# Two idle TensorE products at the start, and VectorE sums in the first three steps of a four-layer attention chain

## The chip, the cores and the metric

The kernel runs on one core of a Trainium2 chip. TensorE multiplies matrices into PSUM, VectorE (DVE in the profile) and ScalarE (ACT) read PSUM and work between PSUM and SBUF, GpSimd (POOL) does small work, and the sync engine (SP) issues most DMAs. The metric is device time in microseconds, the median of several runs.

## The reference

Four layers are applied in a row to `x` of shape (4, 64, 64, 64), all in float32. Every layer is an attention of 4096 tokens with 64 channels per image. The change touches layer 0 of the first image, which computes

```
q = x @ Wq + bq;  k = x @ Wk + bk;  v = x @ Wv + bv       # per image: 4096 x 64
attn = softmax(q @ k.T, axis=-1)                          # 4096 x 4096, rows sum to 1
out  = attn.T @ v                                         # note the transpose
x    = gamma * out + x
```

Layer 1 is an attention over max-pooled keys with spectrally normalised weights, layers 2 and 3 are attentions after a group norm. They are not touched.

## The kernel before

**Work and order.** `fast_path` writes all work in one order by hand (manual scheduling): every engine runs its instructions in the order in which the Python code issues them. The unit is a `step`. In a step of layer 0, `first` runs twice: each makes one score tile of 128 query rows by 1024 keys (TensorE, line 999, into one of two rotating PSUM buffers `s`) and its exponential on ScalarE. Four score tiles make one block of 128 query rows. Three steps later the products with the values follow (`adds`, line 1028). Between these, `step` calls `advance`, which lets a background generator issue its next piece: projections, values, constants, or parts of another layer. `now[0]` counts the steps since the start of the kernel; layer 0 of the first image has steps 0 to 63.

**The fold of the query and key weights.** The scores are x A x^T with A = Wq Wk^T, so only one projected tensor is needed, in two arrangements called `q` and `q_swapped`; the keys are the transposed input `xT` itself.

**The start.** Before step 0 the code issues, for TensorE in this order: two idle products (`keep_busy`, line 703: zeros times zeros, 128 by 256, into a score buffer that nobody reads), the transposes of Wq and Wk (line 730), one idle product, the product A (line 736), the transposes of the first half of the input (line 930, evacuated by VectorE at line 870 and ScalarE at line 878, one half each), the product for the bias (line 740), one idle product, and the first halves of the two projections (line 891, evacuated at lines 872 and 880). Each float32 product shows as two passes in the profile.

**Steps 0 to 2.** The background pieces are, in step 0, the transposes of the second half of the input, again evacuated by VectorE and ScalarE; in steps 1 and 2, the two halves of the values (line 912, into a score buffer, evacuated with the bias by VectorE at line 916). In a step the two calls of `first` are issued ahead of the background piece:

```python
        if first is not None:
            first()                  # both score tiles, both exponentials
        work = due.pop(now[0], [])   # empty in steps 0 to 2
        ...
        if len(work) < 2:
            advance(MID)             # the background piece
```

**The row sums.** The softmax needs the sum of each exponential's rows. `first` has two ways for it: ScalarE's accumulator beside the exponential (line 1009), or an exponential without it (line 1006) and a sum on VectorE (line 1007). It takes the second where the background waits at a place called `LATE` or `END`, which in layer 0 happens for a part of the second image. After the fourth tile of a block, VectorE adds the four columns (line 1011) and takes the reciprocal (line 1012); ScalarE scales the values with it (line 1017) from step 3 on.

Of the kernel before, what the change touches and what calls it, by code (L numbers as in the profile page):

```python
# [597 lines left out]
def fast_path(tc: tile.TileContext, a: dict, out: bass.AP, bad, read_flag):  # L598
# [9 lines left out]
    nc = tc.nc  # L608
# [3 lines left out]
    P = 128  # L612
# [7 lines left out]
    MID, ALONE, LATE, END = range(4)  # L620
# [8 lines left out]
    s_tile = lambda: ps_s.tile([P, 1024], FP, tag="s", name="s")  # L629
# [67 lines left out]
    idle = scratch[:, 12 * P : 16 * P]  # L697
    nc.vector.memset(idle, 0.0)

    def keep_busy(n):  # L700

        for _ in range(n):
            nc.tensor.matmul(s_tile()[:, 0:256], idle[:, 0:P], idle[:, 0:256], start=True, stop=True)

    load_form(0, 0, a["L0_conv_Wq"], a["L0_conv_Wk"])
    load[:] = [nc.sync.dma_start]
# [27 lines left out]
    def form_product(n, t):  # L734

        nc.tensor.matmul(t, form[n][2][:, 0, :], form[n][2][:, 1, :], start=True, stop=True)
# [5 lines left out]
    def form_scaled(n, i, t, factor):  # L742
        nc.vector.tensor_scalar(blocks[n][i], t, factor, None, ALU.mult)
# [12 lines left out]
    def check_columns(n):  # L756
        i = checks[0]
        checks[0] += n
        return all_z[:, i : i + n], all_r[:, i : i + n]
# [16 lines left out]
    now = [0]  # L776
# [3 lines left out]
    back = {"gen": iter(()), "at": None, "credit": 0.0, "tempo": 1.0, "alone": -1}  # L780
# [35 lines left out]
    def step(first=None):  # L816
        back["credit"] = min(back["credit"] + back["tempo"], 3.0)
        for f in before.pop(now[0], ()):
            f()
        if first is not None:  # L820
            first()
        work = due.pop(now[0], [])
        for n, f in enumerate(work[:2]):
            if n == 1:
                advance(MID)
            split = n == 1 and ready(LATE)
            f(lambda: advance(LATE)) if split else f()
        for f in work[2:]:
            f()
        if len(work) < 2:  # L830
            advance(MID)
            advance(LATE)
        passes = list(later)
        later.clear()
        for f in passes:
            f()
        advance(END)
        now[0] += 1
# [7 lines left out]
    def parts(within, whole):  # L846

        if within is None or whole:
            yield slice(0, 512)
            if within is not None:  # L850
                within()
        else:
            yield slice(0, 256)
            within()
            yield slice(256, 512)

    def banks(on):

        if on == "both" and now[0] < 2:
            bank = [acc_tile(), acc_tile()]  # L860
            return bank, bank
        s = s_tile()
        bank = [s[:, chunk(i)] for i in range(2)]
        return bank if on == "both" else s, bank

    def evacuate(on, dst, src, bias=None):

        if on == "DVE":
            if bias is None:
                nc.vector.tensor_copy(dst, src)  # L870
            else:
                nc.vector.tensor_scalar(dst, src, bias, None, ALU.add)
        elif on == "both":
            m = dst.shape[-1] // 2
            evacuate("DVE", dst[:, 0:m], src[0], bias)
            evacuate("ACT", dst[:, m:], src[1], bias)
        elif bias is None:
            nc.scalar.copy(dst, src)
        else:
            nc.scalar.activation(dst, src, AF.Identity, bias=bias)  # L880
# [42 lines left out]
    def transposed(on, st):  # L923
        xin = st.pop("xin")
        xT = st["x"] = x_tile("xT")
        for g in range(2):
            yield MID
            s, bank = banks(on)
            for i in range(8):
                nc.tensor.transpose(bank[i // 4][:, ds(i % 4 * P, P)], xin[:, g * 8 + i, :, :].rearrange("p i c -> p (i c)"), ident)  # L930
            evacuate(on, xT[:, wide(g)], s)
# [24 lines left out]
    def first_queries(st):  # L956

        st["q"] = x_tile("q"), x_tile("q_swapped")
        st["v"] = x_tile("v").rearrange("p (j f) -> p j f", f=C)
        A, col = blocks[0]  # L960
        st["todo"] = [project("both", q, A, st["x"], col, exchanged=n == 1) for n, q in enumerate(st["q"])]
        for g in st["todo"]:
            next(g)
        yield from first_half(st)
# [13 lines left out]
    def layer0(st):  # L978

        q, k, v = st.pop("q"), st["x"], st.pop("v")
        pairs = NB * NC // 2
        acc, ps, zs, scaled = {}, {}, {}, {}
        zsum, rz = check_columns(NB)

        def queries(m, i, e):

            c, n = divmod(m // 2, 4)
            return q[(c + i) % 2][half(i), ds(c // 2 * 1024 + m % 2 * 512 + n * P + e * C, C)]  # L990

        def first(u):
            m, c = divmod(u, NC)
            if c == 0:
                zs[m] = small.tile([P, NC], FP, tag="z0", name="z0")
            s = s_tile()
            for i in range(2):
                for e in range(2):
                    nc.tensor.matmul(  # L999
                        s[half(e), chunk(i)], queries(m, i, e), k[half(i), chunk(c)], start=True, stop=True  # L1000
                    )
            p = ps[u] = p_tile()
            z = zs[m][:, c : c + 1]
            if back["at"] in (LATE, END):

                nc.scalar.activation(p, s, AF.Exp)
                nc.vector.tensor_reduce(z, p, AX.X, ALU.add)
            else:
                nc.scalar.activation(p, s, AF.Exp, accum_out=z)  # L1009
            if c == NC - 1:  # L1010
                nc.vector.tensor_reduce(zsum[:, m : m + 1], zs.pop(m), AX.X, ALU.add)  # L1011
                nc.vector.reciprocal(rz[:, m : m + 1], zsum[:, m : m + 1])

        def scale(t):
            m = 2 * t // NC
            vs = scaled[t] = z_p.tile([P, C], FP, tag="vs", name="vs", bufs=1)
            nc.scalar.activation(vs, v[:, m, :], AF.Copy, scale=rz[:, m : m + 1])  # L1017

        def add(t, e, n, cols):

            m, second = divmod(2 * t, NC)
            c = (second + 2 * e) % NC + n
            if c not in acc:
                acc[c] = acc_tile()
            for i in range(2):
                nc.tensor.matmul(  # L1028
                    acc[c][half(i), cols], scaled[t][half(e), :], ps[NC * m + c][half(e), chunk(i)][:, cols],
                    start=(m == 0 and not second), stop=(m == NB - 1 and second > 0),  # L1030
                )
                yield

        def adds(t, n, within=None):
            for cols in parts(within, t * 2 < NC or t >= pairs - NC // 2):
                for row_tiles in zip(add(t, 0, n, cols), add(t, 1, n, cols)):
                    pass
            if n == 1:
                del scaled[t]
                if t % 2:  # L1040
                    for u in range(2 * t - 2, 2 * t + 2):
                        ps.pop(u)

        def finish(cs):
            xT = st["x"]
            for c in cs:
                nc.vector.scalar_tensor_tensor(xT[:, chunk(c)], acc.pop(c), gamma0, xT[:, chunk(c)], ALU.mult, ALU.add)
            if not acc:
                st["done0"] = True

        start = now[0]
        for t in range(pairs):
            g = start + t + 3
            before.setdefault(g, []).append(lambda t=t: scale(t))
            due.setdefault(g, []).extend([lambda *within, t=t, n=n: adds(t, n, *within) for n in range(2)])
        due[start + pairs + 2].append(lambda: finish((0, 2, 1, 3)))
        for t in range(pairs):
            step(lambda: (first(2 * t), first(2 * t + 1)))
        return start + pairs + 3
# [516 lines left out]
    def alone(*phases):  # L1576
        background(1.0, *phases)
        drain()

    s0, s1, s2, s3 = state  # L1580
    def rest(phase):
        yield MID
        yield from phase

    keep_busy(2)
    form_transposes(0, s_tile())
    keep_busy(1)
    t = s_tile()[:, 0:P]
    form_product(0, t)
    form_scaled(0, 0, t, 1.0)  # L1590
    st0 = transposed("both", s0)
    next(st0)
    next(st0)
    t = s_tile()[:, 0:1]
    form_bias(0, t)
    form_scaled(0, 1, t, 1.0)
    keep_busy(1)
    alone(first_queries(s0))


# [59 lines left out]
    at = 10 * C  # L1660
# [227 lines left out]
```

## Time and profile before

| What | Value |
|---|---|
| Runs | 2926.57, 2926.76, 2927.2 us |
| Median | 2926.76 us |
| Profiled execution, from the first to the last instruction | 2927.0 us (the page names no other time for it) |
| TensorE matmul busy | 2895.3 us, 99% |
| VectorE busy | 1871.5 us, 64% |
| ScalarE busy | 1800.3 us, 62% |
| Mean granted TensorE clock | 0.998 |

Times are microseconds from the first instruction. In the profile PE is TensorE's matmul, PEld its weight load; a line such as L999 is a line of the kernel. An arrow `out<-in` names the tiles, and a bracket behind a row of the timeline gives the idle time before it and what ended it. "xcount" merges several instructions into one row.

### The profile page before, as it was taken

What the parts mean: (1) busy time and instruction counts of PE and PEld (TensorE: products, weight loads), DVE (VectorE), ACT (ScalarE), POOL (GpSimd) and SP (SyncE); (2) the same over time, 40 slices, a digit from 0 to 9 for tenths busy, and PEclk for the clock granted to TensorE, in tenths of its full rate; (3) what the DMA queues carried; (4) which work ended last, traced back from release to release, by engine and by line L of the source; (5) the groups of instructions that cost most, each with busy time, mean ns of one, the idle gap of its engine ahead of it and who ended that gap; (6) DMA issues with size and microseconds to landing.
All of it is one profiled execution on the core that took longest, in us unless ns stands there. A gap on an engine that the chain in (4) does not pass through costs nothing.

```text
span 2927.0 us, 66546 instructions
## 1 busy us (share of the span) xinstructions
PE 2895.3 (99%) x29397; PEld 1113.6 (38%) x29397; DVE 1871.5 (64%) x2141; ACT 1800.3 (62%) x2481; POOL 35.2 (1%) x35
## 2 busy tenths in 40 slices
PE   9999999999999999999999999999999999999998
PEld 3333233333444433344443343333344444443333
DVE  2111753589821078963027897888888877878878
ACT  5666666665566766566766655555555655555554
POOL 0000000000000000000000000000000000000000
PEclk9999999999999999999999999999999999999999
DMA  2010000000001000000000000000000000000000
GB/s 38 1 30 7 1 1 16 7 5 5 19 5 30 1 7 5 5 23 16 1 1 7 5 9 19 19 5 9 5 19 8 20 5 8 6 20 5 8 5 10
DMA packets 85513, 30.64 MB, mean 10 GB/s; under 512 B 79168, under 2 KB 83264, under 8 KB 83808
## 3 DMA queue, kind: packets, MB, share of 16 engines
q1 hardware_dynamic: 83168, 25.87, 4.8%
q8 instruction: 232, 3.80, 0.6%
q10 hardware_dynamic: 1984, 0.38, 0.1%
q14 instruction: 65, 0.53, 0.1%
q0 software_dynamic: 64, 0.07, 0.0%
HBM read 4.79 MB, written 4.19 MB: 3 GB/s over the span
## 4 chain that ended last, share of the span: by engine, by line
PE 97%; DVE 1%; ACT 1%; issue 0%; DMA 0%; POOL 0%; ACTq 0%; DVEq 0%
PE acc L1323 30%; PE s L1288 30%; PE s L999 15%; PE acc L1028 15%; PE s L1122 2%; PE acc L1148 2%; ACT p L1128 1%; DVE zacc L1299 1%; PE s L1148 1%; PE s L891 0%; PE s L912 0%; PE s L1419 0%; PE s L1467 0%; PE s L1092 0%; PE s L1194 0%
## 5 line engine op out<-in xcount | busy, mean ns | idle before, releaser
L1293 ACT ACTIVATE p<-s 128x1024 f32<-128x1024 f32 x1024 | 994.6, 1022 | 696.2 <-PE s L1288 676.5
L1299 DVE TENSOR_TENSOR zacc<-zacc,p 128x1024 f32<-128x1024 f32 x960 | 1174.2, 1223 | 179.7 <-ACT p L1293 114.8
L1323 PE MATMUL acc<-p,v 64*64 64x512 f32 (+1 forms) x8576 | 1006.6, 573 | 0.0
L1009 ACT ACTIVATE p<-s 128x1024 f32<-128x1024 f32 x480 | 487.3, 1020 | 114.8 <-PE s L999 114.6
L1323 PEld LDWEIGHTS acc<-p,v 64*64 64x64 f32 x8576 | 340.4, 133 | 545.1 <-issue 545.1
L1028 PE MATMUL acc<-p,vs 64*64 64x512 f32 (+1 forms) x4224 | 501.4, 577 | 0.0
L1288 PE MATMUL s<-q,k 64*64 64x512 f32 x2048 | 491.6, 590 | 2.1 <-ACT p L1128 2.1
L999 PE MATMUL s<-xT,q 64*64 64x512 f32 x2048 | 487.2, 591 | 2.4 <-DVE mean L1355 0.7
L1288 PE MATMUL s<-q,xT 64*64 64x512 f32 x2048 | 489.5, 591 | 0.0
L999 PE MATMUL s<-xT,q_swapped 64*64 64x512 f32 x2048 | 487.6, 591 | 0.3 <-DVE o L1157 0.3
L1288 PE MATMUL s<-q,h_swapped 64*64 64x512 f32 x2048 | 481.0, 591 | 3.9 <-DVE v L916 3.5
L1288 PE MATMUL s<-q,k_swapped 64*64 64x512 f32 x2048 | 480.4, 590 | 0.0
L1011 DVE TENSOR_REDUCE all_z<-z 128x1 f32<-128x4 f32 x128 | 20.1, 157 | 606.5 <-ACT p L1009 606.2
L1028 PEld LDWEIGHTS acc<-p,vs 64*64 64x64 f32 x4224 | 173.3, 133 | 266.0 <-issue 264.2
L1288 PEld LDWEIGHTS s<-q,h_swapped 64*64 64x64 f32 x2048 | 145.5, 133 | 144.5 <-issue 131.7
L1288 PEld LDWEIGHTS s<-q,k_swapped 64*64 64x64 f32 x2048 | 148.1, 133 | 137.6 <-issue 87.2
L999 PEld LDWEIGHTS s<-xT,q_swapped 64*64 64x64 f32 x2048 | 146.2, 133 | 141.8 <-issue 110.3
L1288 PEld LDWEIGHTS s<-q,xT 64*64 64x64 f32 x2048 | 145.7, 133 | 138.1 <-issue 131.7
L999 PEld LDWEIGHTS s<-xT,q 64*64 64x64 f32 x2048 | 144.2, 133 | 139.3 <-issue 110.8
L1288 PEld LDWEIGHTS s<-q,k 64*64 64x64 f32 x2048 | 148.6, 133 | 116.7 <-issue 96.2
L1017 ACT ACTIVATE vs<-v,all_r 128x64 f32<-128x64 f32 x256 | 89.1, 348 | 157.2 <-PE acc L1028 80.3
L1128 ACT ACTIVATE p<-s 128x1024 f32<-128x1024 f32 x128 | 124.1, 1022 | 82.4 <-PE s L1122 78.5
(213 smaller groups left out, 1319.6 us busy)
## 6 DMA issues: line engine op xcount, KB each, us to landing
k_swapped<-k SPq DMA_DIRECT2D x8, 512.0 KB, 5.8
residual<-turned SPq DMA_DIRECT2D x128, 32.0 KB, 1.9
h_swapped<-xT SPq DMA_DIRECT2D x8, 512.0 KB, 5.3
out_dram<-turned SPq DMA_DIRECT2D x60, 64.0 KB, 2.0
xin<-in_x_dram SPq DMA_DIRECT2D x12, 256.0 KB, 6.8
q_swapped<-q SPq DMA_DIRECT2D x6, 512.0 KB, 5.5
pg<-pg SPq DMA_DIRECT2D x8, 128.0 KB, 2.3
xin<-in_x_dram SPq DMA_DIRECT2D x12, 64.0 KB, 2.4
```

Source lines behind the costliest of these rows:

```text
L999: nc.tensor.matmul(s[half(e), chunk(i)], queries(m, i, e), k[half(i), chunk(c)], start=True, stop=True)
L1009: nc.scalar.activation(p, s, AF.Exp, accum_out=z)
L1011: nc.vector.tensor_reduce(zsum[:, m : m + 1], zs.pop(m), AX.X, ALU.add)
L1017: nc.scalar.activation(vs, v[:, m, :], AF.Copy, scale=rz[:, m : m + 1])
L1028: nc.tensor.matmul(acc[c][half(i), cols], scaled[t][half(e), :], ps[NC * m + c][half(e), chunk(i)][:, cols], start=(m == 0 and not second) ...
L1122: nc.tensor.matmul(ss[e][half(m), chunk(i)], pgs[0 if e == d else 1][r, ds(n * P + m * C, C)], th[r, chunk(i ^ j)], start=True, stop=True,)
L1128: nc.scalar.activation(pk[e], ss[e], AF.Exp)
L1148: nc.tensor.matmul(acc[quarter(q), :], g[:, k, :], ps[j, k][q // 2][:, chunk(q % 2)], start=(k == 0 or not bank), stop=(k == NK - 1 or not ...
L1288: nc.tensor.matmul(s[half(e), chunk(i)], k[(j + i) % 2][half(i), ds(j // 2 * P + e * C, C)], q[half(i), chunk(c)], start=True, stop=True,)
L1293: nc.scalar.activation(p, s, AF.Exp)
L1299: add = lambda: nc.vector.tensor_tensor(zaccs[c], p0, p, ALU.add)
L1323: nc.tensor.matmul(accs[c][e][half(i), cols], v[half(e), j, :], p[half(e), chunk(i)][:, cols], start=(j == 0), stop=(j == NB - 1),)
```

## The change

The idle product ahead of the first projection is left out. A shorter one, of 128 columns, is put between the product A and the transposes of the input. And in the steps 0, 1 and 2 (six score tiles), the row sums are made by VectorE instead of ScalarE's accumulator.

```diff
-    def keep_busy(n):
+    def keep_busy(n, cols=256):
 
         for _ in range(n):
-            nc.tensor.matmul(s_tile()[:, 0:256], idle[:, 0:P], idle[:, 0:256], start=True, stop=True)
+            nc.tensor.matmul(s_tile()[:, 0:cols], idle[:, 0:P], idle[:, 0:cols], start=True, stop=True)
...
             z = zs[m][:, c : c + 1]
-            if back["at"] in (LATE, END):
+            if back["at"] in (LATE, END) or now[0] < 3:
 
                 nc.scalar.activation(p, s, AF.Exp)
                 nc.vector.tensor_reduce(z, p, AX.X, ALU.add)
             else:
                 nc.scalar.activation(p, s, AF.Exp, accum_out=z)
...
     form_product(0, t)
     form_scaled(0, 0, t, 1.0)
+    keep_busy(1, P)
     st0 = transposed("both", s0)
     next(st0)
     next(st0)
     t = s_tile()[:, 0:1]
     form_bias(0, t)
     form_scaled(0, 1, t, 1.0)
-    keep_busy(1)
     alone(first_queries(s0))
```

## The prediction

> **What bounds the kernel now.** I read the page first (busy shares, then the chain that ended last).
>
> ```profile
> PE 97%; DVE 1%; ACT 1%; issue 0%; DMA 0%; POOL 0%; ACTq 0%; DVEq 0%
> ```
>
> TensorE carries 97% of the chain, and by the page's first part it is busy for 99% of the span (2895.3 us). So nothing on VectorE or ScalarE counts as such; only what makes TensorE start later counts, and it then moves the whole rest. The edits touch the first 30 us alone, so next I read the chain of waits from 0 to 60 us.
>
> ```profile
> 8.63 1.15 PE s L703 x2
> ...
> 16.80 0.70 DVE xT L870
> ...
> 21.22 1.24 DVE v L916
> ...
> 24.69 1.24 DVE v L916
> ...
> 25.97 1.09 PE s L999 x8
> 27.06 0.86 PE acc L1028 x8
> ```
>
> Ahead of the gapless stretch VectorE holds the chain three times: the copy of the second half of the transposed input (16.80), and the two evacuations of the values (21.22 and 24.69). From 25.97 on it is TensorE without a gap. The 1.15 us of L703 at 8.63 is the idle product that the change takes out. Third, the timeline (start, length, engine), for the order of the queues and for prices:
>
> ```profile
> 8.15 0.59 ACT L878 COPY xT<-acc 128x512 f32<-128x512 f32 x1 [3.05 <-PE acc L930]
> ...
> 15.37 1.02 ACT L1009 ACTIVATE p<-s 128x1024 f32<-128x1024 f32 x1 [1.18 <-PE s L999]
> ...
> 16.38 1.02 ACT L1009 ACTIVATE p<-s 128x1024 f32<-128x1024 f32 x1
> ```
> ```profile
> 291.43 1.94 ACT L1006 ACTIVATE p<-s 128x1024 f32<-128x1024 f32 x2
> ...
> 292.48 2.35 DVE L1007 TENSOR_REDUCE z<-p 128x1 f32<-128x1024 f32 x2 [7.54 <-ACT p L1006]
> ```
>
> The second fence is the branch that the change extends, as layer 0 of the second image already runs it: two exponentials without the accumulator take 1.94 us (one per 0.92 us; with it 16.38 - 15.37 = 1.01), the first sum starts 1.05 us after its exponential, one sum takes 1.21 us, and two in a row 2.35 (1.14 apart).
>
> **Part 1, the idle products.** Removed: two passes of 256 columns, 1.15 us on the chain at 8.63 to 9.78. Under them lies the next wait: the projection (L891) reads both halves of xT, and ScalarE's copy of the second ends at 8.15 + 0.59 = 8.74. So without them it could start at 8.79 instead of 9.71, a gain of 0.92, not 1.15. Added: two passes of 128 columns after the weight product (L736, which ends at 5.93) and ahead of the transposes. The trace has no such product; the nearest rows are the transposes, also 128 columns and 128 weights (8 started over 7.69 - 6.14, 0.22 apart, so 0.44 for two), and half of the 256-column pair (0.58). The transposes start at 6.14 after an idle 0.21 us, a wait for the input's DMA, which hides part. What remains, 0.23 to 0.37, delays the transposes, both copies and the projection; below, 0, if the weight loads overlap more. I take 0.25, near the transposes' row. Gain 0.92 - 0.25 = 0.67, less 0.02 for start-up: **-0.65** (from -0.92 to -0.5). Both products are written to a rotating score buffer; as many are taken as before. The bias product now gets the other one, last read by the scaling at 5.97 to 6.26, long before 8.04.
>
> The clock could spoil this. The projection's passes start 0.85 us apart (10.62, 11.47), later ones 0.43: TensorE speeds up between 13.2 and 14.2. The granted clock's record says 1.00 there, so I go by the pace. The scores wait for q_swapped's evacuation (13.44 to 14.19, at L999 14.24); with the shift that is 13.59. If the rise comes 4.9 us after dense work begins, as from 8.63 to about 13.5, it comes at 9.06 + 4.9 = 13.96 and costs (13.96 - 13.59) / 2 = 0.2. By the longest row (5.87, below) it comes at 14.9 and costs 0.65. I take 0, since the dense work itself comes earlier, and keep 0.65 for the range. The Trainium skill, "TensorE: Matmul & The Clock Gate", section "Part 1", ties the rise to a free-running window of about 3.4 us; by it, as an estimate, one window missed would cost up to 1.7 us in place of my 0 to 0.65.
>
> **Part 2, the sums.** Removed: six accumulator reads (0.19 us each) on ScalarE, which isn't on the chain; each second exponential of a pair starts 0.09 earlier. Added: six VectorE sums of 1.21 us, 7.3 us in all, in the stretch where VectorE is mostly idle. But VectorE works in order, and in each step both sums are issued ahead of the background piece. Each sum waits for an exponential, and behind it waits what TensorE needs next. No DMA moves and no queue of SP or POOL is passed. In times of the trace of before:
>
> Step 0: exponentials at 15.37 and 16.29. Sums 16.42 to 17.63 and 17.56 to 18.77. The xT copy, which started at 16.80, starts at 18.70 and ends at 19.39; L999 starts 0.14 after it, as now: 19.53 against 17.64, **+1.89**.
>
> Step 1: exponentials at 19.53 + 1.15 = 20.68 and 21.60. Sums from 21.73 and 22.87, the second until 24.08. The two small column steps (sum and reciprocal, 0.2 us apart) now wait for it; the evacuation (L916) starts at 24.40 instead of 21.22: +3.18, a further **+1.29**. It frees the score buffer that the sixth score tile takes: 25.68 for 22.50.
>
> Step 2: the sixth exponential at 23.65 + 3.18 = 26.83, its sum 27.88 to 29.09 (the fifth's ends at 26.78). The second L916 starts at 29.02 instead of 24.69: +4.33, a further **+1.15**. The eighth score tile takes its buffer at 30.30 for 25.97; the output products follow directly. Nothing later in the chain has slack against the start, so the 4.33 stays to the end. Bounds: 3.9 if each sum hands over 0.07 earlier, 4.7 if semaphores add as much.
>
> **Sum.** The page names only the span as the profiled execution's time, 2927.0; 2927.0 - 0.65 + 4.33 = 2930.68. The median of the runs is 0.24 below that span, so I forecast 2926.76 + 3.68 = **2930.4 us**, +0.13%. About 0.2% (5.9 us) is what a measurement of this kernel can tell from no change. The likeliest case's own range is 2929.7 (-0.92, +3.9) to 2931.6 (-0.5, +4.7, +0.65).
>
> **Rivals.** *Slower by more: the clock falls in the new gap.* TensorE now idles from about 17.2 to 19.53, 2.3 us. Stretches of the trace (us, then busy time of PE, PEld, DVE, ACT, POOL, then the granted clock):
>
> ```profile
> 166.00:168.00 2.00, 0.65 (x27) 0.38 (x20) 0.05 (x1) 0.00 (x0) 0.00 (x0) 1.00 0.41 53
> ```
> ```profile
> 1785.00:1786.00 1.00, 0.86 (x8) 0.00 (x0) 0.90 (x2) 0.09 (x1) 0.00 (x0) 1.00 0.00 0
> ...
> 1788.40:1788.60 0.20, 0.00 (x0) 0.00 (x0) 0.20 (x1) 0.00 (x0) 0.00 (x0) 0.58 0.00 0
> ```
> ```profile
> 1795.20:1795.40 0.20, 0.20 (x8) 0.05 (x4) 0.00 (x0) 0.00 (x0) 0.00 (x0) 0.85 0.00 0
> ```
>
> An idle 1.35 us kept the full clock; TensorE idle from 1785.86 lost it at 1788.43, after 2.57 us, and had it back at 1795.26, 5.87 us after work resumed at 1789.39. A gap of 2.3 us lies just short. If the clock falls at its end for that stretch's 6.83 us, the score tiles of steps 1 and 2 take 1.72 for 0.86; most of that hides behind VectorE's sums, and the sixth tile's 0.9 stays. If the recovery waits for the gapless work from 30 on, half of those 6.83 us again at half clock adds 1.7: +2.6 in all, 2933.0. It decides from 2.2 us on (2932.6). The skill's rule (same page, "Why this matters for your kernels") asks for no idle gap above about 3 us; by it this gap costs nothing. The trace's own 2.57 us is stricter.
>
> *The sums are hidden*, VectorE being two tenths busy here: then only -0.65 stays, 2926.1. It needs the xT copy ahead of the sums; the order of issue is against it. *A later fall is missed:* the 6.83 us at half clock around 1790 cost TensorE 5.87 / 2 = 2.9. If the shift moves the fall away, 2927.5; VectorE's wait there is unchanged, so little speaks for it.
>
> **How the numbers follow.** Forecast 0.60, clock falls 0.27 (two thirds of it above 2932.6), sums hidden 0.04, later fall missed 0.09. Range 2927.3 to 2933.8: it takes the forecast's own range, the third rival (2927.5), and the first (2931.3 with the 0.9 alone, 2933.0 with both terms) with 0.8 above for the sizes (0.4 of the sums, 0.4 of the rise). Faster by over 0.2%: 0.01. Slower: 0.18 from the first rival and 0.03 from sizes, 0.21. Within: 0.78.
>
> **What would show it.** Right: six L1007 sums of 1.21 us before 30 us, VectorE's copy of xT near 18.1 (18.70 - 0.65), L916 near 23.8 and 28.4, the projection at 9.06, and a page otherwise shifted by 3.7 us. Wrong: the copy ahead of the sums; score passes 0.85 apart after 18 us (first rival); a projection that doesn't start earlier.

## The result, and the profile after

The changed kernel takes 2931.59 us (median of 21 runs, 2928.40 to 2933.53) against 2926.73 us before (21 runs, 2924.20 to 2928.00). The ratio is 1.0015, with a 95% interval of 1.0010 to 1.0021: slower by 4.9 us, less than the 0.2% that counted as a difference in the forecast. The profiled execution lists 2931.83 us for a span of 2930.1, so 1.7 us lie around the span, and it is a typical one. By the same 1.7 us the profiled execution of before (span 2927.0) took about 2928.7, 2.0 above its median; I had no such number when I set the span beside the median.

The chain of waits of the changed kernel, 0 to 60 us (start, length, what):

```profile
5.94 0.72 PE s L703 x2
...
8.88 3.63 PE acc L891 x16
...
15.54 2.35 DVE z L1007 x2
17.88 0.61 DVE xT L870
18.49 0.14 issue
18.62 3.40 PE s L999 x16
...
23.10 1.23 DVE z L1007
...
24.63 1.24 DVE v L916
...
28.12 1.22 DVE z L1007
29.34 1.14 DVE v L916
...
30.53 1.09 PE s L999 x8
31.62 0.86 PE acc L1028 x8
```

The short idle product of the forecast's part 1 is at 5.94, the projection starts earlier, and from 15.54 on the chain runs through VectorE's sums (L1007) three times, ahead of the xT copy and of both evacuations L916. The eighth score tile starts at 30.53 instead of 25.97: 4.56 us late. One thing in these rows is not a matter of order: the 16 score passes of step 1 take 3.40 us, where they took 1.95. Busy times in stretches of the same run (PE, PEld, DVE, ACT, POOL, then the granted clock):

```profile
17.00:18.00 1.00, 0.00 (x0) 0.00 (x0) 1.00 (x2) 0.00 (x0) 0.00 (x0) 1.00 0.17 40
18.00:19.00 1.00, 0.38 (x4) 0.24 (x8) 0.48 (x1) 0.00 (x0) 0.00 (x0) 1.00 0.18 41
19.00:20.00 1.00, 1.00 (x9) 0.33 (x5) 0.00 (x0) 0.00 (x0) 0.00 (x0) 0.50 0.12 10
...
22.00:23.00 1.00, 1.00 (x65) 1.00 (x59) 0.62 (x1) 0.95 (x1) 0.00 (x0) 0.80 0.19 45
```

TensorE stands still in the gap that the sums open (from 16.31, when the transposes end, to 18.62), and at 19.0 the clock falls to half until 22.4. Two rows from the stretch where layer 3 begins, where before had its own fall from 1788.43 to 1795.26:

```profile
1793.00:1794.00 1.00, 0.28 (x4) 0.21 (x8) 1.00 (x2) 0.00 (x0) 0.00 (x0) 0.96 0.00 0
...
1797.00:1798.00 1.00, 1.00 (x12) 0.42 (x8) 1.00 (x2) 0.00 (x0) 0.00 (x0) 0.83 0.00 0
```

Here the fall runs from 1793.92 to 1797.34, 3.4 us instead of 6.8. TensorE works at half clock for 3.4 us instead of 5.87, which gives back (5.87 - 3.4) / 2 = 1.2 us. The first passes of layer 3 start at 1793.72 instead of 1789.39, 4.33 us late, and 4.33 - 1.2 = 3.1 us is what is left between the two spans. The shorter fall is chance: in the second profile of the same kernel, below, it lasts 6.83 us. So the medians, 4.9 apart, are the better measure.

### The profile page after: what moved, and what is told of

Read it like the earlier page. It is cut to its first block, busy times and chain, and to the rows that moved or that the text cites. A ratio compares the mean times of both kernels' runs of the same rounds, so it can differ in the third digit from the quotient of the medians.

```text
span 2930.1 us, 66548 instructions
## 1 busy us (share of the span) xinstructions
PE 2894.7 (99%) x29397; PEld 1124.5 (38%) x29397; DVE 1878.6 (64%) x2147; ACT 1799.3 (61%) x2475; POOL 35.2 (1%) x35
## 4 chain that ended last, share of the span: by engine, by line
PE 96%; DVE 2%; ACT 1%; issue 0%; POOL 0%; DVEq 0%
PE acc L1323 30%; PE s L1288 29%; PE s L999 15%; PE acc L1028 15%; PE s L1122 2%; PE acc L1148 2%; DVE zacc L1299 1%; ACT p L1128 1%; PE s L1148 1%; PE s L891 0%; PE s L1419 0%; PE s L912 0%; PE s L1467 0%; PE s L1092 0%; PE s L1194 0%
## 5 line engine op out<-in xcount | busy, mean ns | idle before, releaser
L1011 DVE TENSOR_REDUCE all_z<-z 128x1 f32<-128x4 f32 x128 | 20.1, 157 | 603.4 <-ACT p L1009 603.1
```

## The experiments

Theory A: the sums cost because of their place in VectorE's order (4.3 us), and the gap that they open costs the clock as well; the idle products gain 0.9 us. Theory B: the missing idle product costs the clock, and the sums are nearly free. Theory C: the sums cost by themselves, wherever they stand. The kernel before, run beside them, took 2926.66 us (33 runs) in the first group, 2927.06 (27) in the second and 2927.00 (21) in the third; these agree within 0.4 us, so versions of different groups are compared too. Where medians are too coarse I give the difference of the means, with a 95% interval from resampling the runs.

**Only the idle products changed.**

```diff
-            if back["at"] in (LATE, END) or now[0] < 3:
+            if back["at"] in (LATE, END):
```

> Only the idle products are changed; the sums stay on ScalarE's accumulator. Theory A (the sums on VectorE cost 4.3 us of order and about 1.1 us of clock, the products gain 0.9): the first projection at 8.81 as in the changed kernel, all later work 0.9 us earlier than before, 2925.8 us. Theory B (the missing idle product costs the clock, and the sums are nearly free): slower than before by 3 us or more, score passes 0.85 us apart somewhere after 14 us.

Measured: 2925.91 us (11 runs), ratio 0.9998 (0.9989 to 1.0007); difference of the means -0.50 us (-1.25 to 0.27). The projection starts at 8.81 and the passes of step 1 take their old 1.95 us (the chain of waits):

```profile
16.95 1.95 PE s L999 x16
```

Theory B falls. The products' gain is small, and by the runs not clear of zero.

**Only the sums moved.** The diff is the branch of the change alone, with the idle products as before.

> Only the sums of steps 0 to 2 move to VectorE; the idle products are as before. Theory A: the xT copy starts at 18.70, the gap of TensorE ahead of it is 2.3 us; with the clock kept 2926.7 + 4.3 = 2931.0, with a fall of the clock in the gap up to 2932.5. Theory B: within 1 us of before.

Measured: 2931.73 us, ratio 1.0016 (1.0007 to 1.0025); difference of the means 4.66 us (3.87 to 5.39). The whole loss is the sums'. In the profile the clock falls from 15.3 to 18.7, after a gap that began at 13.7:

```profile
15.00:15.50 0.50, 0.00 (x0) 0.00 (x0) 0.50 (x2) 0.00 (x0) 0.00 (x0) 0.83 0.09 23
18.50:19.00 0.50, 0.50 (x8) 0.00 (x0) 0.00 (x0) 0.50 (x1) 0.00 (x0) 0.76 0.09 20
```

**The same sums, behind the background piece.**

The list `later` is worked off at the end of each step, behind the background piece; `sum_columns` holds the two small column steps.

```diff
...
+            if now[0] < 3:
+                nc.scalar.activation(p, s, AF.Exp)
+                later.append(lambda: nc.vector.tensor_reduce(z, p, AX.X, ALU.add))
+                if c == NC - 1:
+                    later.append(sum_columns)
+                return
...
```

> The changed kernel, but in steps 0 to 2 each step's two sums (and the two column steps) are issued behind the background piece, so that the xT copy and the evacuations of the values stand ahead of them on VectorE; as many sums, as long. Theory A: the copy starts as soon as its transposes are done, no gap above 0.5 us, and the time is that of the products alone, 2925.8 (a little less, as each second exponential starts 0.09 earlier). Theory C (the sums cost by themselves, through the buffers or the memory they read): still 2929 or more.

Measured: 2925.64 us, ratio 0.9998 (0.9989 to 1.0007); difference of the means to the changed kernel -5.42 us (-6.34 to -4.45). Its chain of waits:

```profile
15.57 0.70 DVE xT L870
16.27 0.14 issue
16.41 1.95 PE s L999 x16
...
19.89 1.23 DVE v L916
21.12 2.26 DVE z L1010 x2
...
23.76 1.13 DVE v L916
```

The copy stands ahead of the sums again, and step 1 runs at full clock. Two sums (L1010 here) still stand ahead of the second L916, since step 1's sums now come before step 2's evacuation; that costs some tenths. Six sums of the same length cost nothing that the runs can tell (-0.05 us against the products alone, -1.06 to 0.98): theory C falls, the order is the cause.

**Only step 0's sums on VectorE.**

```diff
-            if back["at"] in (LATE, END) or now[0] < 3:
+            if back["at"] in (LATE, END) or now[0] < 1:
```

> The changed kernel, but only step 0's two sums are on VectorE (the condition is now[0] < 1); steps 1 and 2 use the accumulator. Theory A (each step adds its own delay: 1.89, 1.29, 1.15): the xT copy is 1.89 us late as in the changed kernel, the evacuations of the values add nothing: with the products' 0.9 and no fall of the clock 2926.7 + 1.0 = 2927.7, with a fall in the 2.3 us gap up to 1.5 more, 2929.2. If one late copy already cost all of it, 2931.6.

Measured: 2928.97 us, ratio 1.0006 (0.9997 to 1.0015); difference of the means 1.64 us (0.72 to 2.60). The chain of waits:

```profile
14.34 2.35 DVE z L1007 x2
16.68 0.61 DVE xT L870
17.30 0.14 issue
17.43 3.69 PE s L999 x16
21.12 1.74 PE s L912 x64
```

The late copy is there, and the fall of the clock behind it (3.69 us for the 16 passes); L916 starts at 22.89, straight after its products, with no sum ahead of it. The fall lasts longer than in the changed kernel, 6.8 us, from 16.6 to 23.4:

```profile
16.50:17.00 0.50, 0.00 (x0) 0.00 (x0) 0.50 (x2) 0.00 (x0) 0.00 (x0) 0.60 0.08 20
23.00:23.50 0.50, 0.50 (x8) 0.00 (x0) 0.50 (x1) 0.00 (x0) 0.00 (x0) 0.57 0.01 2
```

Steps 1 and 2 make up the rest of the loss: the changed kernel's mean is 2.61 us higher (1.52 to 3.65), and the forecast's sum has 1.29 + 1.15 = 2.44 for them.

**The gap filled with idle products.**

```diff
             evacuate(on, xT[:, wide(g)], s)
+        if on == "both":
+            t = acc_tile()
+            for _ in range(3):
+                nc.tensor.matmul(t[:, 0:256], idle[:, 0:P], idle[:, 0:256], start=True, stop=True)
```

> The changed kernel with three idle products of 256 columns right behind the second transposes, into an accumulator bank, so that TensorE's gap of 2.3 us from 16.3 to 18.6 holds about 1.7 us of work; nothing that is waited for changes. Theory A with its clock term: the clock stays up, the sixteen passes of step 1 take 1.95 us as before the change and not 3.40, and the eighth score tile starts about 1.1 us earlier than in the changed kernel (29.4 against 30.53); 2930.5. If the clock has no part in it: no change, 2931.6.

Measured: 2929.72 us, ratio to before 1.0011 (1.0002 to 1.0020); difference of the means to the changed kernel -1.52 us (-2.51 to -0.56). The lines shift by four, so L1003 is the score product and L1011 the sum; L935 is the added product. Its chain of waits, two rows of the timeline and a stretch:

```profile
15.04 2.35 DVE z L1011 x2
17.38 0.61 DVE xT L870
17.99 0.14 issue
18.13 1.12 PE s L1003 x8
```
```profile
15.65 1.46 PE L935 MATMUL acc<-scratch 128*128 128x256 f32 x6
18.13 0.65 PE L1003 MATMUL s<-xT,q 64*64 64x512 f32 x2 [1.01 <-DVE xT L870]
```
```profile
19.00:20.00 1.00, 1.00 (x12) 0.18 (x4) 0.00 (x0) 0.73 (x1) 0.00 (x0) 1.00 0.06 13
```

The sums and the wait for the copy are all there; only TensorE has something to do for 1.46 us of the gap, and the clock stays up. That separates the two parts of the loss: about 1.5 us of clock, and the order, 4.3 us by the traces (by the runs, this version against the products alone, 3.85 us, 2.78 to 4.88). The idle time left, 1.0 us, did not lose the clock.

**The changed kernel once more**, for a second profile.

> The changed kernel once more, for a second profile. If the fall of the clock at 19 us depends on where TensorE's idle time lies in a period that runs on its own, the fall, the first rise (near 13) and the rise after 1794 lie elsewhere against the kernel's start, and the span differs by up to 2 us; if it depends on the gap alone, the fall is at 19.0 again.

Measured: 2930.86 us in one run. Its chain of waits, and two stretches:

```profile
12.69 2.35 DVE z L1007 x2
15.04 0.61 DVE xT L870
15.64 0.14 issue
15.78 3.36 PE s L999 x16
```
```profile
15.00:15.50 0.50, 0.00 (x0) 0.00 (x0) 0.50 (x2) 0.00 (x0) 0.00 (x0) 0.69 0.09 23
18.50:19.00 0.50, 0.50 (x12) 0.09 (x5) 0.12 (x1) 0.35 (x1) 0.00 (x0) 0.90 0.09 23
```

The work of the start lies 2.8 us earlier than in the first profile, because here TensorE was at full speed from about 5 us on and not from about 12 (in the first profile the projection's passes start 0.85 us apart up to 11.43, and the score passes from 12.23 on 0.43 apart); what follows is the same: the sums, the late copy, and a fall from 15.2 to 18.6. It begins 1.7 us after TensorE went idle (13.5), in the first profile 2.7 us after (16.3 to 19.0), when work had even resumed. So the fall is not tied to the length of the gap alone. Slices of 0.2 us give each fall to about 0.02 us. In all four profiles with a fall at the start, the fall near layer 3 begins 1774.93 us after it (19.00 and 1793.93; 15.18 and 1790.12 here; 15.33 and 1790.26 with only the sums moved; 16.60 and 1791.53 with step 0 alone), although the first falls lie up to 3.8 us apart; and each of these falls lasts 3.41 us or twice that. This is what a period would give that runs on by itself, at another place in each execution, and at whose ends the clock can change.

Ahead of layer 3, TensorE idles 3.53 or 3.54 us in all nine profiles in which that gap is not filled. In this one the clock then falls for 6.83 us (1790.12 to 1796.94), in the first profile of the same kernel for 3.41, and with the sums behind not at all:

```profile
1780.00:1800.00 20.00, 16.47 (x268) 6.95 (x263) 13.97 (x13) 9.08 (x11) 0.00 (x0) 1.00 0.01 2
```

Four of the nine fell for 6.8 us, four for 3.4, one kept the clock. So of the 2.8 us that this execution is ahead, 1.0 is left in the span (2929.1 against 2930.1).

**No idle product at all at the start** (sums on ScalarE).

```diff
     form_scaled(0, 0, t, 1.0)
-    keep_busy(1, P)
     st0 = transposed("both", s0)
```

> The sums stay on ScalarE, the idle product ahead of the projection is left out, and the short one ahead of the transposes too. The transposes wait for the input's DMA again and start at 6.14 instead of 6.46, the projection at about 8.55 instead of 8.81: 0.26 us less than with the short one, 2925.6. If the short product earns more than it costs by an earlier rise of the clock, more than 2925.9.

Measured: 2925.99 us, ratio 0.9996 (0.9987 to 1.0005); difference of the means -1.02 us (-1.61 to -0.43). The projection starts at 8.47. Against the version with the short product (-0.50, -1.25 to 0.27) the intervals overlap: that the short one costs its 0.3 us is likely by the trace and not settled by the runs.

**The clock kept at the start of layer 3** (clock_kept; with the idle products of the change, the sums on ScalarE).

```diff
+    t = acc_tile()
+    for _ in range(5):
+        nc.tensor.matmul(t[:, 0:256], idle[:, 0:P], idle[:, 0:256], start=True, stop=True)
     background(0.6, before3("ACT", s1))
     free = layer3(s0, free)
```

> Only the idle products of the change (sums on ScalarE), and five idle products of 256 columns where layer 3 of the first image begins, into an accumulator bank, where TensorE else idles from 1785.9 to 1789.4 and the clock then falls. If the fall there costs what the forecast put on it (5.87 us at half clock, 2.9 us), the clock stays at 1.00 there and the time is 2925.9 - 2.9 = 2923.0. If the idle products delay the first score tiles by as much, no change or slower, 2926 to 2928.

Measured: 2924.26 us (2923.52 to 2925.81), ratio 0.9991 (0.9982 to 1.0000); difference of the means -2.69 us (-3.22 to -2.12). The chain of waits, where before had 1.98 us for the 8 passes and 3.41 for the next 16:

```profile
1788.31 1.09 PE s L1288 x8
1789.40 1.72 PE acc L1323 x16
```

The kernel **with those five products alone**, on the kernel before (clock_alone):

> The kernel before with only the five idle products where layer 3 of the first image begins. If the clock's fall there is what costs, 2 to 3 us less than before (2924 to 2925) and no fall of the granted clock between 1780 and 1800; if the gain of the kernel with both edits came from the start, no change.

Measured: 2925.56 us, ratio 0.9995 (0.9986 to 1.0004); difference of the means -1.65 us (-2.22 to -1.14), and no fall between 1780 and 1800.

**Both gains together**: those five products, and no idle product ahead of the projection or the transposes.

> The kernel before without the idle product ahead of the projection, with nothing ahead of the transposes, and with the five idle products where layer 3 of the first image begins. If the two gains add up (about 1.0 without the product, about 2.1 for the clock kept, by the means of the runs so far), 2924.0 or a little less; if the missing product costs a late rise of the clock, not below 2924.3.

Measured: 2924.86 us, ratio 0.9993 (0.9984 to 1.0002); difference of the means -2.17 us (-2.52 to -1.78). The two gains, 1.02 and 1.65, make 2.67; with their intervals the runs don't settle whether they add up (the difference is 0.5 us, -0.3 to 1.3). Its chain of waits shows something that can eat a gain at the start:

```profile
18.89 1.09 PE s L999 x8
19.98 0.92 PE s L912 x61
20.90 2.14 issue
23.04 0.27 PE s L912 x2
```

This execution was 22.50 - 18.89 = 3.6 us ahead of before at the sixth score tile and is 25.97 - 24.69 = 1.3 ahead at the eighth; most of the lead is the clock's and not the edit's, since clock_alone, with the start of before, has 22.50 - 19.15 = 3.35 of it. It lost the rest within the second half of the values' products: TensorE pauses 2.14 us after 61 of 64 small products, waiting for nothing that the profile shows. The pause is there in the four profiles that reach this place before 22.5 us, and ends at nearly the same time whenever it begins: 22.25 to 22.66 without a product, 22.30 to 23.38 in clock_kept, 21.15 to 23.15 in clock_alone. Before reaches the place at 24.6 and has none. So in these profiles what is gained ahead of it is capped. The DMA view has one lead: a single packet of 0.02 MB on the queue it calls `q8 instruction` lies 2.2 to 2.4 us ahead of the pause's end in each of the four (at 20.8, 20.4, 21.05 and 20.75 us: both gains, no product, clock_kept, clock_alone). That would fit a wait for TensorE's next instructions, but no run changed it: the cause is not shown. Of all versions clock_kept and this one are the fastest, and the runs don't tell them apart (0.6 us by the medians of two groups).

## Why the prediction was right or wrong

The time (2930.4 forecast, 2931.59 measured, inside 2927.3 to 2933.8 and at the top of the likeliest case's 2929.7 to 2931.6) and the side were right, and by the trace the delay by the order of the sums to 0.01 us; two smaller terms were off, and they partly cancel, which is luck.

- *The sums, step 0: +1.89 forecast.* With the start 0.89 earlier, the xT copy would have started at 16.80 - 0.89 = 15.91; it starts at 17.80: 1.89 late. Reading VectorE's queue in the order of issue, with the price of a sum from the second image, was enough.
- *Steps 1 and 2: +3.18 and +4.33 forecast.* The evacuations are late by 24.63 - (21.22 - 0.89) = 4.30 and 29.26 - (24.69 - 0.89) = 5.46. Both are 1.12 to 1.13 above the forecast, so the second's own addition (1.16 against 1.15) was right; the 1.12 came into step 1 with the clock, not with VectorE.
- *The clock term, taken as 0: mis-sized.* The rival "the clock falls in the new gap" got 0.27; the clock fell in all four profiles with the gap unfilled (at 15.2, 15.3, 16.6 and 19.0), and cost 1.1 us in the profile and 1.5 (0.6 to 2.5) by filling the gap. The step that failed is reading "lost after 2.57 us idle" as a bound that a gap of 2.3 us stays below. The four profiles show falls 1.5 to 2.7 us after TensorE's last work ahead of the gap. So the likeliest case was the forecast's sum plus the lower end of that rival, not either alone. Its 2.6 us, with a recovery only after 30 us, came in no profile.
- *The rule of the skill.* The Trainium skill, "TensorE: Matmul & The Clock Gate", section "Why this matters for your kernels", asks for no idle gap above about 3 us. A gap of 2.3 us lost the clock here each time it was left empty; one of 1.0 us kept it. By that measurement about 3 us is too generous, and no length of a gap is a safe rule: 3.5 us of idle time kept the clock in one of nine profiles. One thing is open: right ahead of the 2.3 us TensorE does nothing but transposes (1.09 us, from 15.22 on in the first profile). Whether these count as work for the clock no run here shows; if not, the gap is 3.4 us and the rule holds for it. The same page's section "Part 1" describes a free-running window of about 3.4 us (4096 cycles, 3413 ns). The falls agree with it: 3.41 us long or twice that, 1774.93 us apart, which by the page's figure, as an estimate, is 520 windows, and at other places in each execution.
- *The idle products: -0.65 forecast, -0.89 in the trace.* The transposes were delayed by 6.46 - 6.14 = 0.32, inside the 0.23 to 0.37. The step that failed is the wait taken for the projection: it did not wait for ScalarE's copy, which ends at 8.99, but started at 8.81, straight after the bias product, so its first passes can't need that copy. By the runs the gain is -0.50 us and not clear of zero (-1.02 without any product); that executions which get ahead lose some of it in the pause is possible and not shown.
- *The first rise of the clock, taken as 0.* The forecast let it come 4.9 us after dense work begins. It came at about 12 us in one profile of the changed kernel and at about 5 in the other, so it differs from one execution to the next; no run prices it alone.
- *"A later fall is missed" (2.9 us, 0.09).* In the first profile of the changed kernel it came by half, 3.4 us instead of 6.8, in the second not at all (6.8 us), and with the sums behind there was no fall. Its price was too high as a mean: keeping the clock there gained 1.65 us, since the fall differs from one execution to the next. It belongs in the range of every small change to this kernel, with either sign, and not in a single rival.
- *The sums hidden (0.04)* was rightly low.

## What to carry to other kernels

An engine that idles is not free to take work: what counts is what stands behind the new instructions in its queue, and whether they wait for something late. Issue them behind the work that another engine waits for, and the same six sums cost nothing.

A gap opened on TensorE has two prices, the wait and the clock. Before trusting a bound such as "this gap is shorter than one that lost the clock", look at several executions: here the same gap of 3.5 us kept the clock, lost it for 3.4 us or lost it for 6.8, by its place in what looks like a period that the kernel doesn't control. One profile shows one case.

## What the runs showed of the hardware that was not expected

- TensorE reaches full speed at the start at very different times: by the pace of the passes after 13.2 us in the profile of before, from about 12 in the first profile of the changed kernel, and from about 5 in four others (its second profile, the sums alone, clock_alone, both gains), where the first eight transposes take 1.0 to 1.1 us instead of 1.7 to 2.0. The granted clock's record reads 1.00 through all of it.
- A fall of the clock lasts 3.4 us or 6.8, in no profile anything between (left out is one behind TensorE's last products, which lasts to the end of every profile). It does not follow from the length of the gap alone: the same 3.5 us ahead of layer 3 gave none, 3.4 or 6.8.
- In four profiles TensorE gets to the last of the second half's 64 small products between 20.9 and 22.3 us and passes them only from 22.7 to 23.4; the pause is up to 2.14 us. Its cause is open.
